# Attention and a mixture of experts on one core: which blocks of the softmax rows are turned by VectorE and through DRAM, where q's bias is added, and where the routed rows are kept

## The chip, the cores and the metric

The kernel runs on one core of a Trainium2 chip, written in Bass with the Tile scheduler. The metric is the time of one execution on the device in microseconds, as a median of several runs. One execution was also recorded by the hardware profiler; times of single instructions are from that one.

The core's engines are named as the profile names them: PE (TensorE, matmuls and transposes by matmul; PEld are its weight loads), DVE (VectorE), ACT (ScalarE), POOL (GpSimd), SP (SyncE, which here only issues transfers). Every engine takes its instructions in order. PE writes to PSUM, eight banks of 128 × 512 f32; the other engines read it out.

## The reference, cut to what matters

The input `x` is (1, 2048, 128) in float32. The reference is one pre-LN transformer block:

```
h   = layernorm(x) * g + b
q, k, v = einsum('bse,ehd->bshd', h, qkv_w) + qkv_b      # H = 16 heads, D = 64
l   = q k^T / sqrt(D), masked causally
x1  = x + softmax(l) v  projected by out_w, + out_b
z   = layernorm(x1)
out = x1 + sum over the 2 best of 8 experts of weight * ffn_e(z) + ffn_shared(z)
ffn(z) = (silu(z gate^T) * (z up^T)) down^T              # 352 hidden units
```

Everything is computed in float32. The sequence is 2048 tokens, 16 blocks of 128.

## The kernel before, in words

**Attention.** The 16 heads are taken in 8 pairs j (64 + 64 partitions). For one pair, the 16 query blocks are taken two at a time: step m has the query blocks i = 2m (called q=0) and i = 2m+1 (q=1), and by causality 2m+2 key blocks. The steps of a pair are taken in the order `turns = [2, 7, 0, 6, 1, 5, 3, 4]` (L389), so that a long step stands beside a short one. The 64 steps of all pairs run in one loop (L677 to L748).

A step's scores (`score_units`, L399) are made in chunks of up to four key blocks: two PE matmuls, one per head (L434), into two PSUM banks; then DVE scales each chunk, writes it to the row tile in SBUF and keeps its maximum (L445). The last chunk of a row, with the diagonal, takes the causal mask in the same instruction (L449). When a row is done, DVE makes the negative maximum (L463) and ACT applies the exponential in place and sums it up (L466, one instruction per head). Six PSUM banks (tag "r") serve scores, projections and transposes in turn; two more (tag "av") hold the products.

To multiply by v, the rows must be turned, so that keys lie on the partitions. There are two ways:

- **by PE**: four PE transposes per key block, two query blocks by two heads (two for the last block, which only q=1 reaches), into a PSUM bank (`turn`, L528, the transpose is L534), which ACT copies to SBUF (L537). Steps m = 0 to 3 do this for all blocks, three at a time (tile `pT`).
- **by slabs**: the scores of those blocks are made with the keys in another order, so that a row lies in SBUF as four slabs of 32 keys per block. DVE then turns the row in 32 × 32 squares in place (L508), SP writes it to DRAM in four transfers (L512), and when both query blocks and both heads are there, one transfer brings the whole step back as the tile `turned`, with keys on the partitions (`load_turned`, L515; the transfer is L526). `by_slabs(m)` (L395) says how many of a step's blocks go this way: `(2 * m) // 4 * 4` for m of 4 or more, so 8 of 10 blocks for m = 4, 8 of 12 for m = 5, 12 of 14 for m = 6 and 12 of 16 for m = 7. The rest, the tail with the diagonal blocks, goes by PE (`turn_last`, L539, tile `tail`): 14 PE transposes each for m = 5 and 7, 6 each for m = 4 and 6. Both query blocks of a step have the same number of slabs.

The products with v are `times_v` (L559, L566), the division by the sums is L587 on DVE, with the reciprocals spread over the partitions by small POOL transfers through DRAM (L497, L579); `project` makes the output projection on PE (L593) and adds it to the residual `xr` on DVE (L594).

q, k and v of the next pair are made by `qkv_units`, in units that are put between the steps of this pair: PE makes a quarter (512 tokens, L357), DVE adds q's bias and writes `qT` (L367), ACT adds k's bias (L369), ACT copies v (L381).

**What sets the order.** In the loop PE and DVE follow the order in which the program writes their instructions (`manual_schedule`, L626, for the two engines); the order on ACT, POOL and SP is made by the Tile scheduler. Each step is written in three groups of blocks. For a step by slabs the first group is the tail and the other two are halves of the slab blocks:

```
groups = [list(range(near, 2 * m + 2))]
groups += [list(range(k, k + near // 2)) for k in range(0, near, near // 2)]
```

In each group come, in this order: units of q, k, v; DVE transposes that are due (`turn_slabs`, L481); the products with v; more units; then, in the first group of a step by slabs, `turn_last` of the next step by slabs, and in the second group `load_turned` of the same one; and lastly chunks of scores of a step that is four later. So the scores of a step by slabs are made two such steps ahead, and its load is issued one such step ahead.

**Routing.** In the last pair, when a batch of two steps is projected, `route_units` (L216) makes the second layer norm (ACT, L199, into the tile `row`), the logits, the two best experts, and the place of each token in its expert's list; POOL then scatters the rows of this batch to a DRAM buffer `zbuf`, eight indirect transfers per batch (L330). The four batches are the steps (2, 7), (0, 6), (1, 5) and (3, 4). The tile `row` of batches 0 and 1 lies in the homes of `kT` and `vt`, which the last pair no longer needs; batches 2 and 3 have tiles of their own, `row2` and `row3`, in a pool that lasts. After the attention its pool is given up, and a new pool, `ffn`, takes the same memory for the experts' weights and work tiles. ACT needs its table for the sigmoid loaded anew where it last used the exponential (`ACT_TABLE_LOAD`).

**Experts.** The shared expert is computed while the last batch is routed (L777, L781, L785, L794); when all rows are scattered, 39 blocks of 128 routed rows are loaded (L909), go through their expert (L932 to L980) and are scattered to `ybuf` (L981), from where the results are gathered and added.

Of the kernel before, what the change touches and what calls it, by code (L numbers as in the profile page):

```python
# [16 lines left out]
P = 128  # L17
# [6 lines left out]
def attention_then_moe(  # L24
# [89 lines left out]
    )  # L114

    enum = const.tile([P, 2, NE], F32, name="enum")
    for e in range(NE):
# [232 lines left out]
    def qkv_units(j):  # L350
# [4 lines left out]
        def qk_unit(s, n):  # L355
            pq = psp.tile([P, 512], F32, tag="r", name=f"pq_{j}_{s}_{n}")
            nc.tensor.matmul(  # L357
                pq,
                wq_of[j][:, s, :, :],
                xnT[:, ts(n, 512)],  # L360
                start=True,
                stop=True,
            )
            bias = bqk[:, s, j : j + 1]
            if s == 0:
                qT[n] = pool.tile([P, 512], F32, tag=f"qT{n}", name=f"qT_{j}_{n}", bufs=1)
# [28 lines left out]
    def by_slabs(m):  # L395

        return (2 * m) // 4 * 4 if 2 * m >= NT // 2 else 0

    def score_units(j, m, kT, qT):  # L399

        inv_of[j, m] = small.tile([P, 32], F32, tag="inv", name=f"inv_{j}_{m}", bufs=8)
        nc.gpsimd.memset(inv_of[j, m], 0.0)
        X = by_slabs(m) * 32
        units = []
        rows_of[j, m] = [None, None]
        for q in range(2):
            i = 2 * m + q
            w = (i + 1) * P
            nch = (w + 511) // 512
# [3 lines left out]
            def unit(c, q=q, i=i, w=w, nch=nch, mx=mx, top=top):  # L413
                c0, cw = c * 512, min(512, w - c * 512)
# [22 lines left out]
                for h in range(2):  # L437
                    mh = mx[:, h, c : c + 1]
                    if c < nch - 1:
                        dst, src = rows[:, h, c0 : c0 + cw], scs[h]  # L440
                        if c0 < 4 * X:
                            dst = rows[:, h, : 4 * X].rearrange("p (b x) -> p b x", b=4)
                            dst = dst[:, :, ts(c, P)]
                            src = src.rearrange("p (b x) -> p b x", b=4)
                        nc.vector.tensor_scalar(  # L445
                            dst, src, SCALE, None, ALU.mult, ALU.max, accum_out=mh
                        )
                    else:
                        nc.vector.tensor_tensor_reduce(  # L449
                            out=rows[:, h, c0 : c0 + cw],  # L450
                            in0=scs[h][:, :cw],
                            in1=mask[:, 512 - cw : 512],
                            scale=SCALE,
# [27 lines left out]
    def turn_slabs(most, age=True, due=False):  # L481
# [4 lines left out]
        while to_turn and (to_turn[0][-1] < 0 or not (age or due)):  # L486
# [3 lines left out]
            if h == 1:  # L490
                inv = inv_of[j, m]
                nc.vector.reciprocal(inv[:, 2 * q : 2 * q + 2], sums)
                if q == 1:
# [6 lines left out]
                    )  # L500
            X = by_slabs(m) * 32
# [6 lines left out]
            nc.vector.transpose(row, row)  # L508
            row = row.rearrange("p (b x) -> p b x", b=4)
            to = staged_of[j, m].rearrange("(b i) (c x) -> i b c x", i=32, c=16)  # L510
            for a in range(4):
                ins = nc.sync.dma_start(to[:, :, 8 * q + 4 * h + a, :], row[ts(a, 32)])  # L512
                no_order(f"stage_{j}_{m}", ins)

    def load_turned(j, m):  # L515
        while any(t[:2] == [j, m] for t in to_turn):
            turn_slabs(1, age=False)
        X = by_slabs(m) * 32
        turned_of[j, m] = pool.tile(
            [P, 16 * NT // 4 * 3 * 32],  # L520
            F32,
# [3 lines left out]
        )  # L525
        nc.sync.dma_start(turned_of[j, m][:, : 16 * X], staged_of[j, m])  # L526

# [11 lines left out]
    def turn_last(j, m):  # L539

        tail_of[j, m] = pool.tile([P, 4, 2, 256], F32, tag="tail", name=f"tail_{j}_{m}", bufs=1)
        for b in range(by_slabs(m), 2 * m + 2):
            turn(j, m, b, tail_of[j, m][:, b - by_slabs(m)])

    def turned(j, m, b):
        near = by_slabs(m)
        q0 = 1 if b == 2 * m + 1 else 0
        if b < near:
            t = turned_of[j, m][:, : 16 * 32 * near]
            t = t.rearrange("p (q h a x) -> p h q a x", q=2, h=2, a=4)  # L550
            return j, m, b, q0, t[:, :, :, :, ts(b, 32)]
        if near:
# [6 lines left out]
    def times_v(j, m, b, q0, pT, vt):  # L559

        near = by_slabs(m)
        if b == near:
            av_of[j, m] = psp.tile([P, 256], F32, tag="av", name=f"av_{j}_{m}", bufs=2)
        for h in range(2):
# [4 lines left out]
                pT[:, h],  # L569
                start=(b == near),  # L570
                stop=(b == (near or 2 * m + 2) - 1),
# [105 lines left out]
    for n, (j, m) in enumerate(steps):  # L677
# [399 lines left out]
```

## Time and profile before

| what | value |
|---|---|
| median of 3 runs | 1029.68 us (1029.33 to 1029.85) |
| profiled execution | 1026.97 us, span 1025.2 us |
| mean granted TensorE clock | 0.972 of full speed |
| DMA, queue q1 (SP's transfers) | 118176 packets, 190.65 MB, 60.9% of 16 engines |
| PE transposes of the rows (L534) | 896, mean 279 ns, 119.9 us |
| ACT copies of the tails (L537) | 64 of 128×512 at 589 ns, 32 of 128×256 at 384 ns |
| DVE transposes (L508) | 64 of 128×1024 at 1223 ns, 64 of 128×1536 at 1758 ns |
| DVE, q's bias (L367) | 32 at 748 ns |
| ACT, k's bias (L369) | 32 at 687 ns |
| transfer of one step's slabs back (L526) | 2048 KB for m = 4 and 5, 3072 KB for m = 6 and 7 |

How it is read: a row of the timeline gives the start in us from the span's start, the duration, the engine, the line of the kernel, the operation, what it writes and reads, and how many instructions are put together in the row; in brackets, how long the engine stood idle before it and what ended this. A duration in the timeline is that of the whole row. The table by stage gives busy time and, in brackets, the number of instructions of each engine in a stretch.

### The profile page before, as it was taken

What the parts mean: (1) busy time and instruction counts of PE and PEld (TensorE: products, weight loads), DVE (VectorE), ACT (ScalarE), POOL (GpSimd) and SP (SyncE); (2) the same over time, 40 slices, a digit from 0 to 9 for tenths busy, and PEclk for the clock granted to TensorE, in tenths of its full rate; (3) what the DMA queues carried; (4) which work ended last, traced back from release to release, by engine and by line L of the source; (5) the groups of instructions that cost most, each with busy time, mean ns of one, the idle gap of its engine ahead of it and who ended that gap; (6) DMA issues with size and microseconds to landing.
All of it is one profiled execution on the core that took longest, in us unless ns stands there. A gap on an engine that the chain in (4) does not pass through costs nothing. (4 is left out here: it accounts for less than half of the span.)

```text
span 1025.2 us, 18420 instructions
## 1 busy us (share of the span) xinstructions
PE 947.1 (92%) x5930; PEld 567.2 (55%) x5930; DVE 750.3 (73%) x2359; ACT 541.2 (53%) x1017; POOL 203.5 (20%) x392
## 2 busy tenths in 40 slices
PE   4895899999999999999999999999999887889996
PEld 2462545565555555655565555555555554457774
DVE  3763888778877887787778777877888883655554
ACT  4571446564655565556556654565565552315552
POOL 1030120211111111111111111111111105334441
PEclk9998799999999999999999999999999988989998
DMA  9984849874987488748874887588658863623104
GB/s 215 218 267 123 293 110 307 238 238 128 300 247 223 143 273 256 223 154 261 268 213 161 259 265 210 170 251 259 199 181 271 250 184 121 196 56 86 40 24 130
DMA packets 128030, 205.31 MB, mean 200 GB/s; under 512 B 16864, under 2 KB 120642, under 8 KB 123840
## 3 DMA queue, kind: packets, MB, share of 16 engines
q1 hardware_dynamic: 118176, 190.65, 60.9%
q0 software_dynamic: 8032, 13.22, 5.5%
q8 instruction: 48, 0.79, 0.3%
q10 hardware_dynamic: 1728, 0.27, 0.2%
q14 instruction: 46, 0.38, 0.1%
HBM read 105.10 MB, written 99.35 MB: 199 GB/s over the span
## 5 line engine op out<-in xcount | busy, mean ns | idle before, releaser
L466 ACT ACTIVATE row<-row,neg 128x1920 f32<-128x1920 f32 (+15 forms) x256 | 306.3, 1202 | 201.1 <-DVE neg L463 91.0
L445 DVE TENSOR_SCALAR_CACHE_REDUCE row<-sc 128x512 f32<-128x512 f32 x384 | 243.5, 685 | 90.9 <-PE sc L434 73.6
L434 PE MATMUL sc<-kT,qT 64*128 64x512 f32 (+3 forms) x1280 | 297.8, 554 | 10.2 <-ACT tail L537 4.4
L434 PEld LDWEIGHTS sc<-kT,qT 64*128 64x128 f32 x1280 | 122.5, 187 | 150.0 <-issue 83.2
L508 DVE STREAM_TRANSPOSE row<-row 128x1024 f32<-128x1024 f32 (+1 forms) x128 | 190.3, 1491 | 0.8 <-ACT row L466 0.8
L566 PE MATMUL av<-turned,vt 128*64 128x256 f32 x1280 | 157.2, 393 | 0.0
L449 DVE CUSTOM_DVE_ANT_0 row<-sc,mask 128x384 f32<-128x384 f32 (+3 forms) x256 | 114.9, 485 | 20.3 <-PE sc L434 19.6
L534 PE MATMUL tr<-ident,row 128*128 128x128 f32 x896 | 119.9, 279 | 10.3 <-DVE row L445 6.4
L534 PEld LDWEIGHTS tr<-ident,row 128*128 128x128 f32 x896 | 101.1, 143 | 44.4 <-issue 19.9
L497 POOL DMA_DIRECT2D invd<-inv x60 | 43.2, 720 | 410.9 <-DVE inv L495 287.2
L537 ACT COPY pT<-tr 128x512 f32<-128x512 f32 (+1 forms) x160 | 78.4, 552 | 84.5 <-PE tr L534 79.3
L566 PEld LDWEIGHTS av<-turned,vt 128*64 128x64 f32 x1280 | 88.2, 140 | 62.4 <-issue 23.2
L579 POOL DMA_DIRECT2D inb<-invd x120 | 71.7, 603 | 179.8 <-DMA invd<-inv 114.4
L566 PE MATMUL av<-pT,vt 128*64 128x256 f32 (+1 forms) x640 | 81.4, 378 | 6.3 <-ACT pT L537 5.9
L357 PE MATMUL pq<-xnT,wq 128*128 128x512 f32 x128 | 72.1, 654 | 0.9 <-DVE row L445 0.9
L566 PEld LDWEIGHTS av<-pT,vt 128*64 128x64 f32 x640 | 39.3, 138 | 49.1 <-issue 19.6
L593 PE MATMUL po<-wo,aT 128*128 128x128 f32 x256 | 44.8, 299 | 15.0 <-DVE aT L587 6.3
L593 PEld LDWEIGHTS po<-wo,aT 128*128 128x128 f32 x256 | 34.7, 197 | 33.7 <-DVE row L445 21.6
L537 ACT COPY tail<-tr 128x512 f32<-128x512 f32 x96 | 43.9, 521 | 14.7 <-PE tr L534 14.7
L981 POOL DMA_INDIRECT ybuf<-yo,to x39 | 38.3, 983 | 61.9 <-ACT yo L980 61.9
L466 ACT ACTIVATION_READ_ACCUMULATOR row<-row,neg 128x1 f32 x256 | 49.8, 195 | 0.0
L950 DVE TENSOR_TENSOR hk<-sk,uk 128x352 f32<-128x352 f32 x39 | 20.3, 520 | 36.1 <-PE uk L946 31.2
(169 smaller groups left out, 899.4 us busy)
## 6 DMA issues: line engine op xcount, KB each, us to landing
stage<-row SPq DMA_DIRECT2D x256, 192.0 KB
turned<-stage SPq DMA_DIRECT2D x16, 3072.0 KB
stage<-row SPq DMA_DIRECT2D x256, 128.0 KB
turned<-stage SPq DMA_DIRECT2D x16, 2048.0 KB
zbuf<-mask SPq DMA_DIRECT2D x8, 1056.0 KB
inb<-invd POOLq DMA_DIRECT2D x120, 64.0 KB
zs<-zbuf SPq DMA_DIRECT2D x39, 66.0 KB
yt<-ybuf SPq DMA_DIRECT2D x4, 512.0 KB
```

The source lines that it names most:

```text
L357: nc.tensor.matmul(pq, wq_of[j][:, s, :, :], xnT[:, ts(n, 512)], start=True, stop=True,)
L434: nc.tensor.matmul(sc[:, :cw], qT[i // 4][hd, ts(i % 4, P)], keys, start=True, stop=True)
L445: nc.vector.tensor_scalar(dst, src, SCALE, None, ALU.mult, ALU.max, accum_out=mh)
L449: nc.vector.tensor_tensor_reduce(out=rows[:, h, c0 : c0 + cw], in0=scs[h][:, :cw], in1=mask[:, 512 - cw : 512], scale=SCALE, scalar=-F32_M ...
L466: nc.scalar.activation(row, row, AF.Exp, bias=neg[:, h : h + 1], accum_out=sums[:, h : h + 1])
L497: small_dma(j, m)(invd_of[j, m].rearrange("n (a i) -> a n i", a=4), inv,)
L508: nc.vector.transpose(row, row)
L534: nc.tensor.transpose(tr[:, h, ts(q, P)], rows_of[j, m][q][:, h, ts(b, P)], ident)
L537: nc.scalar.copy(dst[:, :, q0 * P :], tr[:, :, q0 * P :])
L566: nc.tensor.matmul(av_of[j, m][hd, q0 * P :], vt[:, b, hd], pT[:, h], start=(b == near), stop=(b == (near or 2 * m + 2) - 1),)
L579: small_dma(j, m)(inb[h * D : (h + 1) * D, :].rearrange("d (q p) -> d q p", q=2), row.partition_broadcast(D),)
L593: nc.tensor.matmul(po[:, q, :], aT[:, ts(q, P)], wo[:, j, :], start=True, stop=True)
```

## The change

Four edits:

1. **More blocks by slabs.** `by_slabs(m)` becomes `(2 * m + 2) // 4 * 4`: 8 of 10 blocks for m = 4, all 12 for m = 5, 12 of 14 for m = 6, all 16 for m = 7. Steps 5 and 7 have no tail any more, and their three groups are thirds of their blocks (4, 4, 4 and 5, 5, 6). The diagonal blocks of these steps are now in slab order, so the mask is needed in that order too (`mask_s`, built once on POOL).
2. **Rows of different length.** The two query blocks of such a step have a different number of blocks by slabs (`slab(m, q)`): 11 and 12 for m = 5, 15 and 16 for m = 7, in place of 8 and 8, 12 and 12. The DVE transposes and the transfers have these lengths, and the load of m = 5 and m = 7 is two transfers, one per query block. The tile `turned` of odd m grows by a third, the tile `tail` is halved.
3. **q's bias on ACT** for all pairs but the first, in the place of DVE.
4. **Homes of the routed rows.** Batch 2 takes the memory of a row tile of the attention pool (`row2_0`), batch 3 a tile `row` of the `ffn` pool; the tiles `row2` and `row3` go, and a batch's tile is taken when its layer norm is written instead of at the start of its units.

The diff, cut to its core:

```
+    mask_s = const.tile([P, 4, 4, 32], F32, name="mask_s")
+    nc.gpsimd.memset(mask_s, 0.0)
+    nc.gpsimd.tensor_copy(
+        mask_s[:, :, 3, :], mask[:, 384:512].rearrange("p (b i) -> p b i", b=4)
+    )
...
     def route_units(blocks, number):
-        if number < 2:
-            row = pool.tile([P, S], F32, tag=("kT", "vt")[number], name=f"row_{k0}")
-            row = row[:, : n * ROW].rearrange("p (t c) -> p t c", t=n)
-        else:
-            row = norm.tile([P, n, ROW], F32, tag=f"row{number}", name=f"row_{k0}", bufs=1)
+        row = None
+        def home():
+            tag, shape = (
+                ("kT", [P, S]),
+                ("vt", [P, S]),
+                ("row2_0", [P, 2, 5 * P]),
+                ("row", [P, n * ROW]),
+            )[number]
+            t = (pool if number < 3 else ffn).tile(shape, F32, tag=tag, name=f"row_{k0}", bufs=1 + (number < 2))
+            if len(shape) == 3:
+                t = t.rearrange("p h x -> p (h x)")
+            return t[:, : n * ROW].rearrange("p (t c) -> p t c", t=n)
...
         def normed():
+            nonlocal row
+            row = home()
...
-                nc.vector.tensor_scalar_add(qT[n], pq, bias)
+                if j:
+                    nc.scalar.activation(qT[n], pq, AF.Identity, bias=bias)
+                else:
+                    nc.vector.tensor_scalar_add(qT[n], pq, bias)
...
     def by_slabs(m):
-        return (2 * m) // 4 * 4 if 2 * m >= NT // 2 else 0
+        return (2 * m + 2) // 4 * 4 if 2 * m >= NT // 2 else 0
+
+    def slab(m, q):
+        return min(by_slabs(m), 2 * m + q + 1) * 32
+
+    def first_block(m):
+        near = by_slabs(m)
+        return near if near < 2 * m + 2 else 0
...
                 for h in range(2):
                     mh = mx[:, h, c : c + 1]
+                    dst, src = rows[:, h, c0 : c0 + cw], scs[h][:, :cw]
+                    hide = mask[:, 512 - cw : 512]
+                    if c0 < 4 * X:
+                        dst = rows[:, h, : 4 * X].rearrange("p (b x) -> p b x", b=4)
+                        dst = dst[:, :, c * P : c * P + cw // 4]
+                        src = src.rearrange("p (b x) -> p b x", b=4)
+                        hide = mask_s[:, :, 4 - cw // P :, :].rearrange("p b k i -> p b (k i)")
...
             X, Xq = by_slabs(m) * 32, slab(m, q)
...
-            row = rows_of[j, m][q][:, h, : 4 * X]
+            row = rows_of[j, m][q][:, h, : 4 * Xq]
             nc.vector.transpose(row, row)
...
-                ins = nc.sync.dma_start(to[:, :, 8 * q + 4 * h + a, :], row[ts(a, 32)])
+                ins = nc.sync.dma_start(to[:, :, 8 * q + 4 * h + a, :Xq], row[ts(a, 32)])
...
-            [P, 16 * NT // 4 * 3 * 32],
+            [P, 16 * 32 * (NT if m % 2 else NT - 4)],
...
-        nc.sync.dma_start(turned_of[j, m][:, : 16 * X], staged_of[j, m])
+        by_slot = "p (q c x) -> q p c x"
+        into = turned_of[j, m][:, : 16 * X].rearrange(by_slot, q=2, c=8)
+        of = staged_of[j, m].rearrange(by_slot, q=2, c=8)
+        if slab(m, 0) == X:
+            nc.sync.dma_start(turned_of[j, m][:, : 16 * X], staged_of[j, m])
+        else:
+            for q in range(2):
+                Xq = slab(m, q)
+                nc.sync.dma_start(into[q][:, :, :Xq], of[q][:, :, :Xq])
...
     def turn_last(j, m):
-        tail_of[j, m] = pool.tile([P, 4, 2, 256], F32, tag="tail", name=f"tail_{j}_{m}", bufs=1)
+        if by_slabs(m) == 2 * m + 2:
+            return
+        tail_of[j, m] = pool.tile([P, 2, 2, 256], F32, tag="tail", name=f"tail_{j}_{m}", bufs=1)
...
             groups = [list(range(near, 2 * m + 2))]
             groups += [list(range(k, k + near // 2)) for k in range(0, near, near // 2)]
+            if not groups[0]:
+                groups = [list(range(k * near // 3, (k + 1) * near // 3)) for k in range(3)]
```

In `times_v` the first product of a step is found by `first_block(m)` in place of `by_slabs(m)`; in `turned` the last block of a step by slabs takes only its q=1 half. Nothing is changed in the experts.

More of the change, by code (lines that the diff above doesn't have):

```diff
@@ L402, in score_units @@
         nc.gpsimd.memset(inv_of[j, m], 0.0)
-        X = by_slabs(m) * 32
         units = []
@@ L408, in score_units @@
             w = (i + 1) * P
+            X = slab(m, q)
             nch = (w + 511) // 512
@@ L411, in score_units, with unit @@
             mx = small.tile([P, 2, 4], F32, tag="mx", name=f"mx_{j}_{i}", bufs=6)
-            def unit(c, q=q, i=i, w=w, nch=nch, mx=mx, top=top):
+            def unit(c, q=q, i=i, w=w, nch=nch, mx=mx, top=top, X=X):
                 c0, cw = c * 512, min(512, w - c * 512)
@@ L438, in unit @@
                     mh = mx[:, h, c : c + 1]
-                    if c < nch - 1:
[L440 to L444, printed above, removed]
+                    dst, src = rows[:, h, c0 : c0 + cw], scs[h][:, :cw]
[5 more added lines that the diff above has]
+                        hide = mask_s[:, :, 4 - cw // P :, :].rearrange("p b k i -> p b (k i)")
+                    if c < nch - 1:
                         nc.vector.tensor_scalar(
@@ L449, in unit @@
                         nc.vector.tensor_tensor_reduce(
-                            out=rows[:, h, c0 : c0 + cw],
-                            in0=scs[h][:, :cw],
-                            in1=mask[:, 512 - cw : 512],
+                            out=dst,
+                            in0=src,
+                            in1=hide,
                             scale=SCALE,
@@ L500, in turn_slabs @@
                     )
-            X = by_slabs(m) * 32
+            X, Xq = by_slabs(m) * 32, slab(m, q)
             if not X:
@@ L550, in turned @@
             t = t.rearrange("p (q h a x) -> p h q a x", q=2, h=2, a=4)
-            return j, m, b, q0, t[:, :, :, :, ts(b, 32)]
+            return j, m, b, q0, t[:, :, q0:, :, ts(b, 32)]
         if near:
@@ L561, in times_v @@
         near = by_slabs(m)
-        if b == near:
+        if b == first_block(m):
             av_of[j, m] = psp.tile([P, 256], F32, tag="av", name=f"av_{j}_{m}", bufs=2)
@@ L569, in times_v @@
                 pT[:, h],
-                start=(b == near),
+                start=(b == first_block(m)),
                 stop=(b == (near or 2 * m + 2) - 1),
```

## The prediction

> **What bounds the kernel now.** I read the page's first part, then a table of busy time by stage, then one period of the attention loop on the timeline. The profiled execution took 1026.97 us (span 1025.2); the median of the runs shown is 1029.68, so 2.7 us are added to whatever the profile gives. About 0.2% (2 us) is what a measurement of this kernel can tell from no change.
>
> ```profile
> PE 947.1 (92%) x5930; PEld 567.2 (55%) x5930; DVE 750.3 (73%) x2359; ACT 541.2 (53%) x1017; POOL 203.5 (20%) x392
> ```
>
> The table by stage (length, busy time and count of PE, PEld, DVE, ACT, POOL, then granted clock, DMA share and GB/s) shows that all the attention time is alike:
>
> ```profile
> 300.00:400.00 100.00, 97.86 (x640) 56.24 (x640) 79.97 (x237) 57.60 (x104) 16.10 (x32) 1.00 0.71 222
> 400.00:500.00 100.00, 97.86 (x642) 56.36 (x640) 80.04 (x236) 57.54 (x105) 16.24 (x32) 1.00 0.73 225
> ```
>
> A head pair j takes 100 us (the same transfer, the load of m=5's slabs, is issued at 318.96 and 419.39), and there are eight. PE looks like the bound. But its busy time is modelled and hides waits (below, twelve scores are counted as 2.21 us at one place and as 3.85 at another), so 97.86% is no proof. The test is which engine runs without gaps at the places where the change takes PE work out. These are rows of PE, then of DVE:
>
> ```profile
> 312.78 1.69 PE L534 MATMUL tr<-ident,row 128*128 128x128 f32 x14
> 314.40 2.21 PE L434 MATMUL sc<-kT,qT 64*128 64x512 f32 x12
> 365.14 1.75 PE L534 MATMUL tr<-ident,row 128*128 128x128 f32 x14
> 366.82 3.85 PE L434 MATMUL sc<-kT,qT 64*128 64x512 f32 x12
> ```
>
> ```profile
> 313.03 1.20 DVE L508 STREAM_TRANSPOSE row<-row 128x1024 f32<-128x1024 f32 x1
> 315.56 0.69 DVE L445 TENSOR_SCALAR_CACHE_REDUCE row<-sc 128x512 f32<-128x512 f32 x1 [1.33 <-PE sc L434]
> ...
> 363.18 1.74 DVE L508 STREAM_TRANSPOSE row<-row 128x1536 f32<-128x1536 f32 x1
> ...
> 367.98 0.69 DVE L445 TENSOR_SCALAR_CACHE_REDUCE row<-sc 128x512 f32<-128x512 f32 x1 [0.50 <-PE sc L434]
> ```
>
> After both sets of 14 transposes (the tails of m=5 and m=7) come scores that DVE has to take out of PSUM. DVE stood still for only 1.33 and 0.50 us there; else it was late itself: at 366.82 the same twelve scores take 3.85 us instead of 2.21, because DVE frees the banks one by one.
>
> **The change, part by part.**
>
> *PE, removed.* Per j 28 transposes go, 14 of m=5 and 14 of m=7. The group's mean is 279 ns, but they overlap: 1.69/14 = 0.12 us each, so 28 × 0.12 = 3.4 us per j if PE set the pace everywhere. The Trainium skill, "TensorE: Matmul & The Clock Gate", Part 4, gives a transpose some 275 ns in a kernel's context; the row's 279 ns agrees, but as a price it would make 28 × 0.275 = 7.7 us per j, and the 1.69 us for 14 decides against it.
>
> *DVE, longer transposes.* Rows of m=5 grow from 1024 to 1408 and 1536 columns, rows of m=7 from 1536 to 1920 and 2048, two heads each: (384+512) × 2 × 2 = 3584 columns. The two shapes measured (1024: 1223 ns, 1536: 1758 ns) give 1.045 ns a column, so 3.75 us per j, half in each step: 0.40 for each q=0 row, 0.535 for each q=1 row. The Trainium skill, "VectorE: DVE Perf Modes", The three transpose paths, leaves DVE the 32×32 blocks and its rules send 128×128 to TensorE, which speaks against the change; here 128 columns cost DVE 134 ns and PE 120 ns, so per block the trace sees almost a tie, and what counts is which engine has room.
>
> *DVE, removed; ACT, changed.* 28 of 32 additions of q's bias leave DVE (748 ns, 3.0 us per j) and become 28 activations on ACT at about 687 ns (the row of k's bias, same shape). ACT loses the tail copies (6 × 589 + 2 × 384 = 4.3 us) and gains 2.75 us per j, so it has more room in sum. Its order is the problem. In the instruction order of the built kernel, q's third quarter comes on ACT behind both exponentials of row 14:
>
> ```profile
> 348.32 1.90 ACT L466 ACTIVATE row<-row,neg 128x1920 f32<-128x1920 f32 x1 [6.95 <-issue]
> ...
> 350.22 1.88 ACT L466 ACTIVATE row<-row,neg 128x1920 f32<-128x1920 f32 x1
> ```
>
> ```profile
> 351.55 1.99 PE L434 MATMUL sc<-kT,qT 64*128 64x512 f32 x8
> ```
>
> That PSUM bank is the one a score of row 15 takes at 351.55 (PE). Before, DVE emptied it; now ACT is free only at 352.1, and 0.69 later, 352.8, the bank is: 1.25 late on PE, with the projection behind it at 354.83 and DVE's addition of it, and so row 14's transposes. I put +1.1 to +1.4 there, against 0.75 that the missing q-bias gives DVE back, which it cannot use while it waits for those scores. Likewise the copies of m=1's turned blocks come behind the exponentials of row 9 (2 × 1.25); part of this lies in a stall of today (PE waits 0.61 for ACT's tail copy at 341.15), and I take +0.15 to +0.4 at 342.5.
>
> *Sum for m=5's place.* From 307.13 to 314.1 DVE has no gap. The first longer transpose (+0.40, at 304.40) lies in the 1.50 us that it waits at 307.13; the others (0.40 + 2 × 0.535 = 1.47) move its end to 315.7, against the 315.56 at which it starts on the scores. So PE's 1.69 us buys 0 here (−0.4 to +0.15).
>
> *Sum for m=7's place.* Delay +1.4, longer transposes +1.87, less the gaps in which DVE waits for PE afterwards (0.50 at 367.98, 1.28 at 373.64, 0.27 at 374.61, 0.62 at 378.30, together 2.67): +0.6. PE's 1.75 us is what lets these gaps close. With m=5's place and the first 0.15: **+0.75 us per period** (bounds: −3.4 if PE has the say throughout, +2 if no gap closes). Seven periods: +5.
>
> *DMA.* The added columns are written and read back: 3584 × 128 × 4 B = 1.83 MB each way, 10.5 to 12.3 MB. By the trace's packets (1024 B 46 ns, 1536 B 65, median) that is 9.5 us of all 16 engines, so the share goes from 0.71–0.73 to about 0.82–0.85. m=5 and m=7 now need the load for their first group, where before the tail's blocks came first; the slack of m=7's load shrinks from some 12 us to 4–5. I cost it at 0 in the middle (bounds 0 to 3 us per j). Only the first pair shows today what a late transfer costs:
>
> ```profile
> 83.77 0.69 DVE L445 TENSOR_SCALAR_CACHE_REDUCE row<-sc 128x512 f32<-128x512 f32 x1 [6.83 <-DMA stage<-row]
> ```
>
> *Start.* In j=0 the transposes of m=7 need not wait for q (3.66 us at 91.46), but the 4 MB load now holds the first product. −2 (−4 to +1).
>
> *Last pair.* No projections of a next pair fill it; DVE runs without a gap from 802.3 to 814.7 with routing work between, so m=5's +1.87 goes through: +1.5 (0 to 1.9).
>
> *Row homes.* Batch 2's rows move to a tile in the attention pool; the last batch's go to the next pool's tile "row", which lies over it. So the last normalisation waits until batch 2's eight scatters have read their rows:
>
> ```profile
> 888.86 0.97 POOL L330 DMA_INDIRECT zbuf<-row,place  x1 [0.30 <-issue]
> ...
> 898.72 1.00 POOL L330 DMA_INDIRECT zbuf<-row,place  x1 [7.98 <-issue]
> ```
>
> ```profile
> 886.24 1.65 ACT L199 ACTIVATE row<-xr,shift_m,rstd_m 128x128 f32<-128x128 f32 x4 [0.98 <-DVE rstd_m L192]
> ```
>
> A scatter has landed 2.3 us after its issue (the last at 907.83, the load that waits for it issued at 910.13): 888.86 + 2.3 = 891.2 instead of 886.24, +5. Behind this normalisation in ACT's queue stand a table load (1.28) and shared-expert activations, ahead of the logits: +5 to +8 on the last scatter, which releases all 39 routed blocks. I take **+6.7**. Mask, memsets and copies on POOL lie in its 80% idle time: 0.
>
> *Sum*: +5 − 2 + 1.5 + 6.7 = +11.2. 1026.97 + 11.2 = 1038.2 by the profile, **1041** as a median. Own range 1036 to 1048.
>
> **Rivals.**
>
> *A, PE sets the pace after all (faster).* At 312.78 and 365.14 PE gets its work back because DVE's longer transposes slide into the gaps it has. Price: half to all of 3.4 us over 7.85 periods, −13 to −26.5, plus 6.7 − 2 at the ends: 1029.7 − 22 = 1008 for all of it, 1021 for half; I say 1014. For: 97.86% busy. Against: DVE's unbroken stretches before both places. It decides once a period gains over 0.7 us, which pays for the two ends.
>
> *B, the loop breaks even* (the delays on ACT lie in its stalls): only the ends count, 1029.7 − 2 + 6.7 = 1034.
>
> *C, transfers land late.* m=7's first group waits 3 us each period: 1041 + 21 = 1062. For: DMA slices near their limit today, and a load of 4 MB instead of 3. Against: 0.15 of the engines left over, and slack of 4 to 5 us.
>
> *D, no change:* loop even, and the last scatter's delay covered by the shared expert's work on PE, which runs to 910: 1030.
>
> **Chances.** Forecast 0.45, A 0.20, B 0.20, C 0.08, D 0.07. Faster 0.20, within 0.2% 0.07, slower 0.73. The range takes in B, D, the forecast and half of A: 1016 to 1056; it leaves out A's lower half and C, 0.18 or so.
>
> **What would show it.** Right: the period of the load grows from 100.0 to 100.5–101; DVE's gaps at the two places close, and PE's busy share falls to about 95%; the score at 351.55 waits for ACT's q; the last batch's normalisation starts after the last scatter of batch 2, and the first of its own scatters comes 5 to 8 us later relative to that. Wrong: a period below 99.5 (A), a wait of the product for the load (C), or unchanged spacing of the scatters (D). The forecast falls if DVE's gaps take up both the longer transposes and ACT's delay.

## The result, and the profile after

The changed kernel took 1086.87 us (median of 4, 1083.4 to 1090.5) against 1029.51 for the kernel before: ratio 1.0563, 95% interval 1.053 to 1.0596. That is slower, as forecast, but by 57 us where 11 were forecast, and outside the range given. The profiled execution took 1088.08 us, with a span of 1086.1 against 1025.2.

The first part of the page and the row of DMA shares, of the changed kernel:

```profile
PE 952.7 (88%) x5706; PEld 558.9 (51%) x5706; DVE 757.5 (70%) x2331; ACT 533.4 (49%) x981; POOL 203.6 (19%) x394
...
DMA  9995959894988598959886987797679873613103
```

PE has 224 instructions less and yet its busy time has not fallen. The same stages as before:

```profile
300.00:400.00 100.00, 93.50 (x580) 52.22 (x577) 76.52 (x223) 51.24 (x89) 15.69 (x32) 1.00 0.79 243
400.00:500.00 100.00, 92.46 (x588) 51.61 (x586) 74.93 (x213) 54.39 (x97) 14.03 (x28) 1.00 0.80 238
```

In 100 us there are fewer PE, DVE and ACT instructions than before; the DMA share is up from 0.71 to 0.79. The granted clock is still 1.00 in these stages (over the whole execution it is 0.961, before 0.972). The kernel has fewer instructions, but they are also spread over more time, so something holds them up. Two rows of the waits (engine and line, what it waited for, us in total, times, longest) name a transfer. The kernel before waited 15.3 us for such writes on DVE, nearly all of it in the first pair, and never on PE for a load:

```profile
DVE row L475 <- DMA stage<-row: 37.6, 13, 7.0
...
PE av L606 <- DMA turned<-stage: 20.4, 8, 7.8
```

Of these, 21.7 us on DVE (8 waits) and 9.7 us on PE (6 waits) lie in the six periods of the next table; in the kernel before it is 1.4 us on DVE there and nothing on PE.

**Where the 61 us lie.** The load of m=7's slabs is issued once per pair, so its issue times cut the run into pieces. In the kernel before it is issued at 171.92 for the second pair and at 774.24 for the last; in the changed one at 178.44 and 815.26.

| piece | before | after | difference | forecast |
|---|---|---|---|---|
| start, up to the second pair's load of m=7 | 171.9 | 178.4 | +6.5 | −2 |
| six periods, from there to the last pair's load | 602.3 | 636.8 | +34.5 | +5 (seven) |
| one such period | 100.39 | 106.14 | +5.75 | +0.75 |
| last pair, up to m=4's load (844.04, 893.56) | 69.8 | 78.3 | +8.5 | +1.5 |
| from there to the first load of routed rows (910.13, 971.89) | 66.1 | 78.3 | +12.2 | +6.7 |
| the routed blocks | 115.1 | 114.2 | −0.9 | 0 |

### The profile page after: what moved, and what is told of

The parts are those of the page before. It is cut to its first block, busy times and chain, and to the rows that moved or that the text cites. A ratio compares the mean times of both kernels' runs of the same rounds, so it can differ in the third digit from the quotient of the medians.

```text
span 1086.1 us, 17943 instructions
## 1 busy us (share of the span) xinstructions
PE 952.7 (88%) x5706; PEld 558.9 (51%) x5706; DVE 757.5 (70%) x2331; ACT 533.4 (49%) x981; POOL 203.6 (19%) x394
## 4 chain that ended last, share of the span: by engine, by line
PE 36%; DMA 20%; DVE 14%; issue 10%; SPq 9%; ACT 5%; POOL 4%; another core or an unknown queue 1%; POOLq 0%; DVEq 0%; ACTq 0%
PE av L606 13%; PE sc L462 11%; DMA turned<-stage 10%; DMA stage<-row 7%; DVE row L538 6%; SPq L542 6%; ACT row L496 3%; POOL ybuf L1023 3%; PE tr L572 3%; PE pq L373 3%; SPq L729 3%; DVE row L479 3%; DVE row L475 3%; PE po L633 2%; PE pv L393 2%
## 5 line engine op out<-in xcount | busy, mean ns | idle before, releaser
L462 PE MATMUL sc<-kT,qT 64*128 64x512 f32 (+3 forms) x1280 | 316.0, 558 | 16.9 <-ACT vt L400 4.4
L538 DVE STREAM_TRANSPOSE row<-row 128x1536 f32<-128x1536 f32 (+4 forms) x128 | 220.1, 1724 | 0.8 <-ACT row L496 0.8
L462 PEld LDWEIGHTS sc<-kT,qT 64*128 64x128 f32 x1280 | 131.5, 187 | 165.5 <-issue 71.5
L606 PE MATMUL av<-turned,vt 128*64 128x256 f32 (+1 forms) x1536 | 191.9, 398 | 20.4 <-DMA turned<-stage 20.4
L606 PEld LDWEIGHTS av<-turned,vt 128*64 128x64 f32 x1536 | 110.4, 143 | 93.1 <-issue 47.3
L572 PE MATMUL tr<-ident,row 128*128 128x128 f32 x672 | 95.9, 281 | 17.0 <-ACT pT L575 12.0
L572 PEld LDWEIGHTS tr<-ident,row 128*128 128x128 f32 x672 | 76.6, 143 | 53.9 <-ACT pT L575 18.6
L606 PE MATMUL av<-pT,vt 128*64 128x256 f32 (+1 forms) x640 | 78.8, 373 | 8.4 <-ACT pT L575 8.4
L479 DVE CUSTOM_DVE_ANT_0 row<-sc,mask 128x128 f32<-128x128 f32 (+1 forms) x192 | 77.3, 439 | 10.0 <-PE sc L462 9.9
L384 ACT ACTIVATE qT<-pq,bqk 128x512 f32<-128x512 f32 x28 | 18.9, 676 | 65.8 <-PE pq L373 65.8
```

What stands on the lines that cost most here:

```text
L462: nc.tensor.matmul(sc[:, :cw], qT[i // 4][hd, ts(i % 4, P)], keys, start=True, stop=True)
L479: nc.vector.tensor_tensor_reduce(out=dst, in0=src, in1=hide, scale=SCALE, scalar=-F32_MAX, op0=ALU.add, op1=ALU.max, accum_out=mh,)
L572: nc.tensor.transpose(tr[:, h, ts(q, P)], rows_of[j, m][q][:, h, ts(b, P)], ident)
L606: nc.tensor.matmul(av_of[j, m][hd, q0 * P :], vt[:, b, hd], pT[:, h], start=(b == first_block(m)), stop=(b == (near or 2 * m + 2) - 1),)
```

## The experiments

The median of the unchanged kernel differs from one chip to another (1017.7 to 1032), so each run is compared with the kernel before on its own chip, and parts of the loop by the **period**: the mean of the six intervals between m=7's loads, from the second pair on. Of the unchanged loop it was 100.39, 100.28, 100.27 and 100.40 in four traces (before, c0, e2, e8). The granted TensorE clock over the six periods was 1.00 in the traces of before, after, c0, e1, e3, e4, e5, e9, e11, e12, e13 and e14, but 0.98 in e6 and 0.96 in e15 and e17.

### One part at a time

**q's bias alone (e1).** The kernel before, with

```
-                nc.vector.tensor_scalar_add(qT[n], pq, bias)
+                if j:
+                    nc.scalar.activation(qT[n], pq, AF.Identity, bias=bias)
+                else:
+                    nc.vector.tensor_scalar_add(qT[n], pq, bias)
```

> The kernel before with q's bias on ACT for all pairs but the first, and nothing else. Theory T (transfers: the added 1.83 MB each way per pair saturate the DMA engines and make the loop wait for them): no transfer is added, so 1029.5 within 3. Theory Q (the prediction's: q's third quarter behind two exponentials on ACT delays PE by 1.1 to 1.4 per pair, 7 pairs): 1037 to 1040 if it is not absorbed. Theory P (VectorE's relief of 3 us per pair counts): below 1027.

Measured: 1030.2 against 1017.67, ratio 1.0116 (1.0092 to 1.0139); period 102.75, so +2.4 to +2.5. The mechanism of Q is there, and dearer than forecast. Rows of ACT, then of PE:

```profile
350.28 1.90 ACT L469 ACTIVATE row<-row,neg 128x1920 f32<-128x1920 f32 x1 [1.48 <-DVE neg L466]
...
352.17 1.88 ACT L469 ACTIVATE row<-row,neg 128x1920 f32<-128x1920 f32 x1
...
354.05 0.67 ACT L368 ACTIVATE qT<-pq,bqk 128x512 f32<-128x512 f32 x1
```

```profile
352.45 1.12 PE L357 MATMUL pq<-xnT,wq 128*128 128x512 f32 x2
353.50 3.25 PE L437 MATMUL sc<-kT,qT 64*128 64x512 f32 x8
```

PE has made q's quarter by 353.5; ACT takes it out at 354.05, after two exponentials, and eight scores that took 1.99 us in the kernel before take 3.25. The changed kernel shows the same at 368.25, where a score waits for ACT's `qT`.

**Three of the four quarters (e7).** The same with `if j and n != 2:`.

> The kernel before with q's bias on ACT, but the third quarter (the one behind row 14's exponentials) left on VectorE. With all four quarters on ACT the period was 102.75 (before 100.3). Theory Q2 (the third quarter alone is to blame): the period falls back to 100.3 to 100.8. Rival (the other quarters, and the copies that move behind row 9's exponentials, cost as much): 101.5 to 102.5.

Measured: ratio 1.0002 (0.9984 to 1.002); period 100.96. Of the 2.4 to 2.5 us, 1.8 belong to the third quarter alone; the other three, with the copies that the scheduler moves on ACT, cost 0.6 to 0.7, a little more than Q2 said. The whole time did not change: in this trace the start and the end are shorter than in c0 (172.1 against 177.3, 53.6 against 57.2).

**The homes of the rows alone (e2).** The kernel before with the fourth edit.

> The kernel before with the new homes of the routed rows alone. Theory H (the last batch's normalisation waits for the scatters of the batch before it): the first scatter of the last batch comes 9 us later against the last one of batch 2 than before (as in the changed kernel's trace), so 1036 to 1041, all of it after the loop; the loop's period stays at 100.4. Rival: in the kernel before, the shared expert's work hides it, 1030.

Measured: 1033.02 against 1017.67, ratio 1.0149 (1.0127 to 1.0171); period 100.27. As Theory H has it, the loss comes after the loop: 71.1 us from the last load of slabs to the first load of routed rows, against 57.2 for the kernel before on the same chip (c0, below). It is dearer than forecast: 15.4 us, where Theory H's 1036 to 1041 meant 6.5 to 11.5 more than 1029.5.

**Only batch 2 moved (e8).** As e2, but `("row3", [P, n * ROW])` comes from the pool `norm`, as before.

> The kernel before with batch 2's rows in the attention pool's tile, as in the change, but the last batch's rows in a tile of their own, as before. Theory H (the overlap of the last batch's tile with batch 2's costs): all of the loss of the new homes goes, ratio 1.000 within 0.002. Rival (batch 2's home itself costs): ratio 1.005 or more.

Measured: ratio 1.0098 (1.0068 to 1.0127), 67.5 us at the end. Theory H falls in the form I gave it: the last batch's own tile was back, its normalisation ran early, and yet two thirds of the loss stayed (0.98% of 1.49%). Rows of ACT:

```profile
881.32 1.65 ACT L199 ACTIVATE row<-xr,shift_m,rstd_m 128x128 f32<-128x128 f32 x4 [10.14 <-DVE shift_m L193]
891.85 1.28 ACT L796 ACT_TABLE_LOAD   x1 [8.89 <-DMA zbuf<-row,place]
```

Now the shared expert's first sigmoid, with the table load ahead of it, waits 8.89 us for batch 2's scatters. Its output too is a tile of the pool `ffn`, which lies over the memory of the attention pool. So most of the cost comes from batch 2's home itself, also with the last batch's rows elsewhere; PE then stands still for 11.48 us before the last batch's transposes (893.79).

**The kernel before, for its trace (c0).**

> The kernel before, unchanged, for a trace from the same chip as the runs beside it: on one chip so far it took 1017.7 as a median, on others 1029.4. If the 12 us lie in the loop, its period is under 99.5; if they lie after the loop, the period is 100.3 and the scatters of the routed rows come some 10 us earlier against the last load of slabs (64 us from that load to the first load of routed rows where it took 1029).

Measured: 1023.03, period 100.28, and 57.2 us at the end against 66.1 in the profiled execution of the kernel before. So the loop is the same on the two chips and the end differs; the start (177.3 against 171.9) and the last pair (72.2 against 69.8) are longer in c0. The trace of 66.1 has one wait of 9.7 us there, of DVE's division for something that the profile only calls remote; the traces of e1, e2, e3, e4, e7, e8, e9 and c0, all from this chip, have no such wait, those of e5, e6, e12, e13, e14 and the changed kernel have one of 9.3 to 12.5. But e11, from the same chip as e12, has none either, nor have e15 and e17. What it is was not found out.

### The slabs

**Without q's bias (e3).** The changed kernel, q's bias on DVE.

> The changed kernel with q's bias back on VectorE. Theory T: VectorE and ACT are not what the loop waits for, so 1087 within 5. Theory Q: 8 to 10 us less, 1077 to 1079. Theory P: more than 1092, since VectorE gets 3 us per pair back.

Measured: 1069.19, ratio 1.0506 (1.0483 to 1.053) against 1017.67; period 103.42. Against the changed kernel's 106.14 the period falls by 2.7, as e1's 2.4 to 2.5 would have it; the 3.1 us over 100.3 that are left are the slabs' own. The ratio falls less, from 1.0563 to 1.0506, some 6 us where Theory Q had 8 to 10; the two ratios are from different chips.

**Only m=5 (e4).** `by_slabs` as `{4: 8, 5: 12, 6: 12, 7: 12}`, `tail` of four blocks, q's bias on DVE.

> Only step m=5 goes by slabs in full (12 of 12 blocks), m=7 stays with 12 of 16 and its tail; new homes, q's bias on VectorE. Half of the added bytes (0.92 MB each way per pair), half of the longer transposes. Theory T with a threshold (nothing is lost until the engines are full): end 9 plus 0 to 10, 1036 to 1050. Theory V (the cost is VectorE's longer transposes and grows with their length): half of the loop's 47 us, 1038 + 24 = 1062.

Measured: ratio 1.0179 (1.0157 to 1.02), of which the homes are 1.0149; period 100.06. Half of the bytes, with half of the slabs, cost nothing in the loop. V falls. What is left is m=7, or a threshold.

**Short transfers (e5).** The changed kernel; what is written and loaded stops at the lengths of before. The edit, cut to its core, with a remark:

```
+        Xk = min(Xq, 32 * kept(m))          # kept: 8 for m=5, 12 for m=7
-        ins = nc.sync.dma_start(to[:, :, 8 * q + 4 * h + a, :Xq], row[ts(a, 32)])
+        ins = nc.sync.dma_start(to[:, :, 8 * q + 4 * h + a, :Xk], row[ts(a, 32), :, :Xk])
```

> The changed kernel, but the transfers of m=5 and m=7 are as short as before: only 8 (m=5) and 12 (m=7) of the blocks' columns are written to DRAM and loaded, and the products of the blocks left out read the columns of the last loaded block, so the output is not the reference's. VectorE's transposes, PE's order, the thirds, the biases and the homes are those of the changed kernel. Theory T: the loop's loss goes, 1029.5 + 9 (end) - 0 to 20 (PE's transposes are gone): 1018 to 1042. Theory V or Q (VectorE or ACT's order costs): stays above 1070. Theory G (the first group needs the load): also stays, 1070 or more, since the load is still needed for the first group.

Measured: 1057.55 against 1029.35, ratio 1.0277 (1.0244 to 1.031), where the changed kernel has 1.0563; period 102.33, 3.8 less. So T is right that the transfers are the largest part of the loop's loss, wrong that they are all of it: the bias is still in this kernel (102.75 alone), and V or Q and G alone would have kept it above 1070. ACT's order is not quite that of the changed kernel; e9 and e12, below, are the cleaner pair.

**The same, clean of bias and of the last batch's home (e9).** As e5, q's bias on DVE, homes as in e8.

> The slabs' part of the change without its transfers: all blocks of m=5 and m=7 by slabs, but only 8 and 12 blocks' columns are written and loaded, the products of the rest read the last loaded block (so the output is not the reference's); q's bias on VectorE; homes as in e8_own3. What is left is 28 PE transposes and the tail copies per pair less, and VectorE's transposes longer by 3.75 us per pair. Prediction's step (VectorE sets the pace at both places, PE's gain does not count): period 99.7 to 101, ratio 0.995 to 1.006. Theory P (PE's 3.4 us per pair count): period 97 to 98.5, ratio 0.975 to 0.985.

Measured: ratio 1.013 (1.0101 to 1.0159), 1.0098 of it the homes as in e8; period 99.66, so −0.6 against 100.28, just below the forecast of 99.7 to 101. This is all that 28 PE transposes and ACT's tail copies less are worth with DVE's longer ones. Theory P's 3.4 us are not there; the prediction's step holds. But the last pair, from m=7's load to m=4's, takes 76.2 us, against 69.7 in e8 and 69.7 to 72.2 in the four traces of the unchanged loop. DVE is busy 62.0 us there against 59.2 in e8, and the granted clock is 0.92 against 0.95; what the rest of the 4 to 6 us is made of was not followed.

**Later need (e6).** The changed kernel without the two lines for `groups` in thirds, so the first group is empty.

> The changed kernel with an empty first group for m=5 and m=7 and their blocks in two halves, so the load is needed by the second group, as before, not by the first. Theory G (the loss is the cover of the tail that is gone, so the load has less time): 1040 to 1060. Theory T (bytes, whatever is waited for): 1080 to 1090.

Measured: 1091.49, ratio 1.0602 (1.0562 to 1.0641); period 106.56. G falls: no product waits for the load any more, but the wait has moved. Theory T's 1080 to 1090 is missed by 1.5. Rows of the waits:

```profile
DVE row L475 <- DMA stage<-row: 60.8, 20, 8.4
...
ACT row L496 <- DMA stage<-row: 47.7, 7, 11.4
```

DVE now waits for the staging writes, since the row tiles can't take new scores before they are read.

**Short loads, full writes (e11).**

> The changed kernel with q's bias on VectorE and every staging write at full length, but the loads of m=5 and m=7 bring only 8 and 12 blocks' columns back (the products of the rest read the last loaded block, so the output is not the reference's). All transfers: period 103.4; none of the added ones: 99.7. Theory B (what counts is the sum of the bytes): half of the 3.7 us goes or all of it, if the loop only loses beyond a full queue: period 100 to 101.7. Theory W (the staging writes are what VectorE waits for, through the row tiles): 102.5 or more. Theory L (the load of m=7 is what the product waits for): 100.3 or less.

Measured: ratio 1.0272 (1.0243 to 1.0301); period 101.80: of the 3.8 us some 1.6 go with the loads' bytes, the rest with the writes'. Just above Theory B's bounds, and neither W nor L: the transfers cost through two waits at once. In the six periods of this trace PE waits 0.4 us for loads and DVE 21.3 us for staging writes; with the full loads (e3) it is 6.8 and 17.6, with short loads and writes (e9) none of either. PE, DVE and ACT have the same orders in e11 and e3; in e9 ACT's is another in places, so the writes' part is the less sure.

**m=7's bytes alone (e12).** As e9, with m=7's transfers at full length (and the homes of the change).

> The changed kernel with q's bias on VectorE, full transfers for m=7 and short ones for m=5 (8 blocks' columns; the products of the rest read the last loaded block, so the output is not the reference's): the added bytes of m=7 alone. Theory S (a threshold in the sum: m=5's bytes alone cost 0.3, so m=7's alone cost little too): period 99.7 to 100.6. Theory 7 (m=7's transfers are late at their own place, whatever m=5 does): 102 to 103.4.

Measured: ratio 1.0427 (1.0398 to 1.0456); period 103.54, as much as with m=5's bytes too (103.42). So S falls, and it is m=7's transfers at their place. This pair, e9 and e12, is the cleanest: the instruction orders of PE, DVE and ACT are the same in both, and only the transfers of m=7 differ, +3.9 us per period. Of e9, SP's queue and two stretches (DMA share is the last column but one):

```profile
361.80 12.20 SPq L544 DMA_DIRECT2D stage<-row  x16
376.87 0.34 SPq L561 DMA_DIRECT2D turned<-stage  x1
```

```profile
361.00:377.00 16.00, 14.42 (x98) 7.80 (x96) 15.84 (x41) 8.72 (x15) 0.85 (x2) 1.00 0.86 262
377.00:392.00 15.00, 14.02 (x98) 8.28 (x96) 11.91 (x40) 12.35 (x23) 3.15 (x6) 1.00 0.82 295
```

Of e12, the same, and the product that needs the load:

```profile
372.63 15.61 SPq L544 DMA_DIRECT2D stage<-row  x16
388.28 3.38 SPq L567 DMA_DIRECT2D turned<-stage  x2
```

```profile
372.00:388.00 16.00, 14.42 (x98) 7.85 (x95) 15.83 (x42) 8.54 (x15) 0.85 (x2) 1.00 0.92 286
388.00:406.00 18.00, 14.75 (x94) 7.94 (x90) 13.19 (x42) 13.01 (x24) 3.14 (x6) 1.00 1.02 334
```

```profile
406.24 1.95 PE L609 MATMUL av<-turned,vt 128*64 128x256 f32 x16 [2.08 <-DMA turned<-stage]
```

From m=7's first transpose on DVE to its first product it takes 32.0 us in e9 (359.61 to 391.57) and 35.8 in e12 (370.43 to 406.24): the 3.9 lies here. And here the DMA share stands at 1.02 in the 18 us of the load, where the six periods show a harmless mean of 0.76 (e9: 0.71). In four of e12's six periods DVE also waits 3.0 to 3.7 us for staging writes just behind the load's issue; in e9 in none.

**The same with less beside it (e15).** As e12, with `{4: 4, 5: 8, 6: 8}` kept.

> As e12_m7_bytes (m=7's transfers full), but the transfers of m=4 and m=6, which run beside those of m=7, are shortened by four blocks too (4 and 8 blocks' columns; the products of the rest read the last loaded block, so the output is not the reference's). Theory C (in this stretch the DMA engines are full, their share is 1.02 while m=7 is loaded, so others' bytes count as much as its own): period 99.3 to 100.5, and no product waits for the load. Theory K (m=7's own chain of write, load and product is too long, whatever runs beside it): 102 to 103.6.

Measured: ratio 1.0565 (1.0531 to 1.0598); period 106.50, longer than with those bytes, at a DMA share of 0.65 over the six periods. This is neither theory's number, and no verdict: the scheduler orders ACT anew when the sizes of transfers change, and in this kernel the exponentials of row 15 and some copies of v and of turned blocks stand elsewhere in ACT's queue than in e12, so more than the bytes was changed. The granted clock was 0.96, too, where e12 had 1.00: PE is busy 587.1 us in the six periods against 576.7, which makes up to 1.7 us per period, a rough estimate, since a busy PE also hides waits. The waits for transfers did get shorter (9.3 us on DVE and 2.3 on PE, e12: 13.1 and 8.2).

**An earlier load (e17).** As e3, but when both rows of m=7's first query block are staged,

```
+            if m == 7 and q == 0 and h == 1:
+                load_q0(j, m)                # tile and load of q=0; q=1's load stays
```

> The changed kernel with q's bias on VectorE, and m=7's load of the first query block issued as soon as that block's rows are staged, not after all sixteen staging writes; same bytes, and the orders of PE, VectorE, ACT and POOL are those of e3_no_bias (period 103.4). Theory B (bytes: in this stretch the engines are full, 0.92 of them busy while m=7 is staged and 1.02 while it is loaded, so an earlier issue only trades places): period 102.5 to 103.6. Theory K (the chain of write, landing, load and product is too long, and the load can start some 7 us earlier): 100 to 102.

Measured: ratio 1.0776 (1.0758 to 1.0794); period 107.67. K's number falls clearly: the load's first part is issued 13 to 14 us ahead of the second, the products hardly wait for it any more (2.7 us in all, none of it in the six periods), and it is the worst kernel of all. B's direction is right, not its number. Rows of DVE and of PE:

```profile
408.20 0.69 DVE L472 TENSOR_SCALAR_CACHE_REDUCE row<-sc 128x512 f32<-128x512 f32 x1 [7.49 <-DMA stage<-row]
```

```profile
408.95 1.83 PE L459 MATMUL sc<-kT,qT 64*128 64x256 f32 x4 [4.75 <-DVE row L472]
```

The second query block's staging writes now stand behind the load, and DVE waits 7.49 us until its row tiles are read: 52.7 us in six periods, in e3 17.6. So the test of K is not a clean one, since the earlier load made the writes later. The granted TensorE clock was 0.96 over the six periods here; PE is busy 587.5 us in them against 577.5 in e3 at 1.00, so by the same estimate up to 1.7 of the 4.3 us per period may be the clock's.

### A better version

> A version meant to be faster than both: only m=5 by slabs in full, q's bias on VectorE, all routed rows in the homes of before (one buffer of a 128-byte tile less makes room for the mask). The loop of e4 (period 100.05 against 100.3) without the end of the new homes: 7 x 0.25 = 2 us less than before, ratio 0.998, between 0.995 and 1.001. If the new homes were not what cost e4 its end: ratio 1.01 or more.

Measured (e13): 1035.95 against 1030.33, ratio 1.0047 (1.0028 to 1.0065); period 100.59. The end is nearly as before (68.3 us against 66.1), so the old homes are worth what was said, but the loop did not gain, and the last pair took 73.7 us against 69.8. The ratio is outside the range expected.

> As e13, with q's bias on ACT for three of the four quarters (not the third). If VectorE's relief of 2.2 us per pair now counts, since VectorE sets the pace at m=5's place: ratio 0.990 to 0.996. If the delays on ACT outweigh it, as in the kernel before (period +0.6 with these three quarters): 0.999 to 1.004.

Measured (e14): ratio 1.0037 (1.0018 to 1.0057); period 101.15. The delays on ACT outweigh DVE's relief again. No version tried beats the kernel before; e7 equals it.

## Why the prediction was wrong

By its steps, in the order it took them:

- **"PE sets no pace at both places": right.** After the change DVE goes from its longer transposes into the scores without a gap at m=5's place (rows of DVE):

```profile
328.88 1.74 DVE L538 STREAM_TRANSPOSE row<-row 128x1536 f32<-128x1536 f32 x1
330.54 0.65 DVE L475 TENSOR_SCALAR_CACHE_REDUCE row<-sc 128x512 f32<-128x512 f32 x1
```

  The gap of 1.33 us is gone, and PE's twelve scores behind it still end in a wait of 1.15 us for DVE (331.26). At m=7's place, in e12, the scores at 381.17 and 383.83 follow what DVE does before them without a gap too. Net −0.6 per pair by e9, not −3.4. Rival A was wrong. The Trainium skill's rule that sends 128×128 transposes to TensorE ("VectorE: DVE Perf Modes", Rules for kernel authors) finds no support in the six periods of e9: with the slabs' transfers cut, VectorE's way was the shorter by 0.6 us per pair. Over the whole kernel it was no gain, since the last pair took 4 to 6 us longer (ratio 1.013, e8 1.0098).
- **q's bias on ACT: right in place, too small.** 0.75 per period was the net of bias and slabs together, with 1.1 to 1.4 for the third quarter; 1.8 was measured for it, 0.6 to 0.7 for the other three with the copies that move (forecast 0.15 to 0.4 for the copies), 2.4 to 2.7 for all four. So the delay itself was put too small, and the measured sum leaves no room for gaps of 2.67 us behind m=7's place that take it up.
- **Transfers at 0, with 0 to 3 as bounds: this is what failed.** They cost 3.8 us per pair (e5, e9), about two thirds of the loop's loss. The slack of "4 to 5" us was negative, as the first product shows:

```profile
408.27 1.95 PE L606 MATMUL av<-turned,vt 128*64 128x256 f32 x16 [1.76 <-DMA turned<-stage]
```

  The step looked at the mean share, 0.82 to 0.85, and at a single chain, the load's. But the writes have a chain too: a row tile takes new scores only when its writes have read it, and DVE's waits for that (21.7 us in the six periods) are longer than PE's for the loads (9.7 us); e11 puts 1.6 us per period to the loads' bytes and the other 2.1 to the writes'. And the share is a mean over a period with a hole in it. Stages of the changed kernel:

```profile
356.00:360.00 4.00, 4.00 (x25) 2.47 (x26) 3.76 (x15) 0.69 (x2) 0.21 (x1) 1.00 0.00 0
360.00:364.00 4.00, 4.00 (x20) 1.42 (x16) 1.27 (x6) 0.93 (x2) 1.85 (x4) 1.00 0.08 12
364.00:368.00 4.00, 3.89 (x22) 1.65 (x20) 2.88 (x10) 4.00 (x5) 0.90 (x2) 1.00 0.08 26
368.00:372.00 4.00, 3.51 (x19) 2.04 (x20) 2.71 (x9) 1.27 (x3) 0.28 (x1) 1.00 0.96 311
```

  For 12 us of this period almost nothing moves; then m=4's load, m=7's staging and m=7's load follow each other at shares of 0.81 to 1.10 until 408. The hole was in the profile of before as well (shares of 0.02, 0.06 and 0.10 from 340 to 352), and so was the full stretch behind it; the prediction averaged over both. Stages of the kernel before:

```profile
344.00:348.00 4.00, 4.00 (x22) 1.80 (x20) 2.00 (x6) 0.00 (x0) 1.81 (x3) 1.00 0.06 4
348.00:352.00 4.00, 4.00 (x24) 1.66 (x22) 3.42 (x13) 3.68 (x3) 0.57 (x3) 1.00 0.10 33
352.00:356.00 4.00, 4.00 (x30) 2.88 (x27) 3.56 (x12) 1.75 (x5) 0.84 (x2) 1.00 0.78 221
356.00:360.00 4.00, 4.00 (x32) 2.46 (x30) 4.00 (x6) 3.96 (x5) 0.00 (x0) 1.00 0.95 394
```

  Rival C named the place and the load's wait; its price of 3 us was near 3.8, of which the loads are less than half, and its chance of 0.08 was far too low.
- **Last pair: right sign, +1.5 against 8.5** (e9: 4 to 6 without any added bytes). DVE has routing work between the transposes there. In the changed kernel it also waits 2.08 and 5.13 us for staging writes (818.42 and 838.10), which the kernel before does not in its last pair, and the granted clock is 0.90 against 0.95. How the 8.5 us divide was not settled.
- **Homes: right wait, too short.** In the changed kernel (ACT, then POOL):

```profile
944.01 1.65 ACT L205 ACTIVATE row<-xr,shift_m,rstd_m 128x128 f32<-128x128 f32 x4 [18.15 <-DMA zbuf<-row,place]
```

```profile
960.50 1.00 POOL L346 DMA_INDIRECT zbuf<-row,place  x1 [15.13 <-DVE e L901]
```

  The last normalisation waits for batch 2's scatters as forecast (941.26, the last one's issue, and 2.3 us to land make 943.6). The end got longer by 12.2, not 6.7. e8 shows that the prediction's mechanism was too narrow: with the last batch's rows elsewhere, the sigmoid in the next pool waited for the same scatters.
- **Start: −2 forecast, +6.5 measured.** No run settles it. In the four traces of the unchanged loop this piece took 171.9 to 177.5, so much of the 6.5 may be scatter. It took 178.0 to 181.0 in the six traces with m=7's writes at full length and no early load (after, e3, e6, e11, e12, e15; in e11 the load is short, and it is 180.0), and 170.4 to 177.5 in the others without an early load; so what there is lies rather with the first pair's writes than with its load.

In sum, per period: −0.6 (slabs on PE and DVE) + 3.8 (transfers) + 2.5 (bias) = 5.7 of the 5.75 measured. That m=7's transfers cost it is shown by e9 and e12; what stays open is how much of their price is full engines and how much the length of m=7's chain: in e17 an earlier load only traded one wait for another, and e15, which was to take the neighbours away, changed ACT's order and ran at a lower clock as well.

## What to carry to other kernels

Judge added transfers by the stretch in which they must land, not by their mean share: a period with a mean of 0.76 lost 3.9 us, while the 18 us that mattered stood at 1.02. Look at both ends of a transfer: who needs what it brings, and who waits until it has read. When an engine that is 98% busy loses work, look at whose row comes next without a gap; here it was VectorE's, and PE's 3.4 us were worth 0.6. A tile put into memory that a later pool takes over makes work of that pool wait for its last reader (here 8.89 and 18.15 us), and an instruction moved to an engine with room still waits behind what stands ahead of it there.

## What the runs showed of the hardware

The kernel before took 1017.7 and 1021.8 us as medians of two sessions on one chip, 1018.4 on a second and 1029.4 to 1032.0 on three more, with a loop of the same period in the two traces there are (100.28 and 100.39). In these two the end of the attention differs most, 57.2 against 66.1 us, and one of them has a wait of 9.7 us there. So effects of 1% were judged by runs of one chip. And moving transfers ahead is not free: with the same bytes, one load that went ahead of eight staging writes lengthened the period from 103.4 to 107.7, of which up to 1.7 may be the lower clock.
